# A two-layer decoder on one core: pacing of the routed rows, constant products ahead of the first expert block, and parts of four, three and one groups

## Chip, core and metric

One core of one Trainium2 chip runs the whole program. The metric is the device time of one execution in microseconds (us); three timed runs of the kernel before gave a median of 1179.47 us (1178.01 to 1180.00).

## What is computed

The input is 32 sequences of 128 tokens with 128 features, and a context of 32 x 128 x 96. Six residual steps follow each other; each takes a layer norm of `x` (the fifth norms `x` once more as latents) and adds its result to `x`:

```python
x = x + rope_attention(ln(x))               # 16 heads of 8
x = x + cross_attention(ln(x), ctx)         # 16 heads of 8
x = x + gated_experts(ln(x))                # 8 routed, 2 shared, hidden 64
x = x + causal_attention(ln(x))             # 16 heads of 8
x = x + latent_attention(ctx, ln(x), mask)  # 2 heads of 64
x = x + relu_experts(ln(x))                 # 8 experts of 512, the best two of each token
```

The change touches the last step. For a token, `probs = softmax(xf @ router_w + router_b)`, the two greatest are kept and scaled to a sum of one, and the token's output is the gated sum of the two experts `relu(xf @ w1[e] + b1[e]) @ w2[e] + b2[e]`. All of it is in float32.

## The kernel before

**Groups and slots.** The 32 sequences are 8 groups of 4 (`NG = 4`). The order of the work is written out by hand: `at(slot, phase, fn)` files a function, and one loop over slots runs, in each slot, the phases open, pre, the attention products of that slot, inner, turn, turned, mid and post. Each engine takes its instructions in the order in which this loop emits them; a slot is a place in that order and not a length of time. The three attentions fill slots 0 to 191 (64 slots each, 8 for a group), with a tail of six slots. `done(stage, g)` is the slot in which group g leaves an attention: `8 * (8 * stage + g) + 17`; so `done(2, 3)` is 169 and `done(2, 7)` is 201. The other steps are filed beside the attentions, by offsets from `done`.

**Latent attention** of group g starts at `d = done(2, g) + 2` and its routing at `d + 19`.

**Routing** (`plan_route`) is made by units of two groups, (0,1), (2,3), (4,5), and of one, (6,) and (7,). Logits, choice of two experts, gates and ranks follow in neighbouring slots; `places` (L1707 on, on VectorE) turns ranks into row numbers, and `scatter` (L1729, an indirect DMA that GpSimd issues) writes the 128 rows of one sequence and one choice to a table in DRAM, `slots[f]`, sorted by expert. A unit of two groups has 16 scatters and a unit of one has 8, two in a slot.

**Empty rows.** `preset` (L2057, on SyncE's queue) fills `slots[f]` with rows whose target is out of bounds, long before the scatters: 12 DMAs, one in every fourth slot from slot 4.

**Parts.** The expert step runs in three parts: groups 0 to 3, groups 4 and 5, groups 6 and 7. A part has `NB` blocks of 128 rows (39, 23, 23), and its blocks go in pairs (20, 12, 12), one pair a slot:

- `table` (VectorE) turns the counts of rows into an expert and a row for each block
- `fetch` (L1868, SyncE) loads a block of rows, four pairs ahead; it waits for all scatters of its part
- `weights` (L1877 on ScalarE, L1879 on VectorE) copies the expert's first matrix out of `all_w`, which `keep` loads in 8 x 2 DMAs from slot 203 on
- `turn` (L1887 on PE, L1889 on VectorE) transposes the block
- `hidden` (L1897 on PE, L1903 and L1905) and `result` (L1914 on PE, L1921 and L1923) are the two products with their evictions
- `leave` (L1928, an indirect DMA issued by GpSimd) writes the 128 results to `y[f]` by token
- when a part is over, `gather` (L1943) reads both results of each token of a group, `finish` (L1948 on GpSimd, L1949 on VectorE) adds them to `x`, and `store` (L1568) writes the group out. The last part's groups do this after the last slot.

The parts begin in slots 209, 229 and 241; the first pair's `hidden` is two slots later.

**Constant products.** `awake` (L298) multiplies an identity in bfloat16 by itself, 128 x 512, into a bank of the pool `ps_t`, and nothing reads it. The kernel before has 46 of these, all in its first 41 us. From slot 197 on `ps_t` has no other user until the first `result`.

Of the kernel before, what the change touches and what calls it, by code (L numbers as in the profile page):

```python
# [22 lines left out]
P = 128  # L23
# [3 lines left out]
G = B // NG  # L27
# [5 lines left out]


BLOCK = 128
PARTS = [(0, 1, 2, 3), (4, 5), (6, 7)]
ROOM = [NG * S * len(p) for p in PARTS]
NB = [2 * r // BLOCK + E - 1 for r in ROOM]
SLOTS = [E * r + E * BLOCK for r in ROOM]
# [50 lines left out]
def constants():  # L90
# [8 lines left out]
    token = np.zeros((P, 2, B), np.int32)  # L99
    for p in PARTS:  # L100
        b = np.arange(NG * len(p))
# [12 lines left out]
def decoder(ctx: ExitStack, tc: tile.TileContext, a: dict, out: bass.AP):  # L114
    nc = tc.nc
# [6 lines left out]
    ps_t = ctx.enter_context(tc.tile_pool(name="ps_t", bufs=2, space=PSUM))  # L122
# [6 lines left out]
    def bank(pool):  # L129
        return pool.tile([P, 512], F32, tag="bank", name="bank")  # L130
# [112 lines left out]
    ident_b = cpool.tile([P, P], BF16, tag="ident_b", name="ident_b")  # L243
# [3 lines left out]
    def wide(t, shape, axis):  # L247
        return t.unsqueeze(axis).to_broadcast(shape)
# [1318 lines left out]
    def store(g):  # L1567
        nc.sync.dma_start(out[g * NG : (g + 1) * NG].rearrange("b p d -> p b d"), X[g])  # L1568
# [5 lines left out]

    N2 = 2 * NG
    UNITS = [(0, 1), (2, 3), (4, 5), (6,), (7,)]
    UNITS_OF = [(0, 1), (2,), (3, 4)]

    def router(slots, lazy):
        b2 = cpool.tile([E, D], F32, tag="b2", name="b2")  # L1580
# [7 lines left out]
        def plan_route(at, g, t):  # L1588
# [5 lines left out]
            groups = UNITS[q]  # L1594
            f = next(f for f, units in enumerate(UNITS_OF) if q in units)
            before = e_base[f] if q == UNITS_OF[f][0] else carry[q - 1]
# [111 lines left out]
            def places():  # L1708
                place = tile8("place")
                nc.vector.tensor_tensor(  # L1710
                    place, m["rp"][:, : n2 * E].rearrange("p (b e) -> p b e", e=E), wide(before, [P, n2, E], 1), ALU.add
                )
                nc.vector.tensor_tensor(carry[q], m["rp"][:, n2 * E : (n2 + 1) * E], before, ALU.add)
                at2 = small.tile([P, 2, N2], F32, tag="r_at", name="r_at", bufs=2)
                for c in range(2):
                    t = tile8("t")
                    nc.vector.tensor_tensor(t, m["picks"][:, c], place, ALU.mult)
                    nc.vector.tensor_reduce(at2[:, c, :n2], t, AX.X, ALU.add)
                m["ati"] = small.tile([P, 2, N2], I32, tag="r_ati", name="r_ati", bufs=2)
                nc.vector.tensor_copy(m["ati"][:, :, :n2], at2[:, :, :n2])  # L1720
                for c in range(2):
                    t = tile8("t")
                    nc.vector.tensor_tensor(t, m["picks"][:, c], m["e"], ALU.mult)
                    nc.vector.tensor_reduce(m["rows"][c][:, :n2, D + 1], t, AX.X, ALU.add)
                    nc.gpsimd.tensor_copy(m["rows"][c][:, :n2, D].bitcast(I32), token[:, c, NG * groups[0] : NG * groups[0] + n2])

            def scatter(c, n):
                def fn():
                    ins = nc.gpsimd.indirect_dma_start(  # L1729
                        slots[f], bass.IndirectOffsetOnAxis(ap=m["ati"][:, c, n : n + 1], axis=0), m["rows"][c][:, n, :], None,  # L1730
                        bounds_check=SLOTS[f] - 1, oob_is_err=False,
                    )
                    tc.declare_no_dep(ins.ins, group=f"slots{f}", reason="no two tokens have one slot")
                    tc.add_to_no_dep_group(f"slots{f}", ins.ins)
                return fn
# [34 lines left out]
            def ranks():  # L1770
                gates()
                ranks_pe()
                places()

            def gates_over(u):
                def fn():
# [28 lines left out]
                t += 1  # L1805
            at(t + 6, "mid", choose3)
            at(t + 7, "mid", ranks)
            n = 0
            for k in range(n2):
                for c in range(2):  # L1810
                    at(t + 8 + n // 2, ("pre", "inner")[n % 2], scatter(c, k))
                    n += 1
            for u in us:
                at(t + 8 + u, "mid", gates_over(u))
# [4 lines left out]
    def expert_blocks(f, total, lazy):  # L1819
# [117 lines left out]
        def gather(g):  # L1937
            b = (g - PARTS[f][0]) * NG
            last = g in PARTS[-1]
# [13 lines left out]
    def experts(halves, lazy, heads, late):  # L1953

        def beside(at, done):
            def swap():
                heads.close()
                lazy["blocks"] = late.enter_context(tc.tile_pool(name="blocks", bufs=3, reuse_waits="tile"))

            def keep(e):  # L1960
                def fn():
                    rows = a["w_f"][e * P : (e + 1) * P]
                    if e == 0:
                        for tag, n in (("w1", W1), ("w2", 512)):
                            lazy[tag] = lazy["blocks"].tile([P, E * n], F32, tag=tag, name="all_" + tag, bufs=1)
                    nc.sync.dma_start(lazy["w1"][:, e * W1 : (e + 1) * W1], rows[:, :W1])
                    nc.sync.dma_start(lazy["w2"][:, e * 512 : (e + 1) * 512], rows[:, W1:])
                return fn

            at(done(2, G - 1) + 2, "open", swap)  # L1970
            for e in range(E):
                at(done(2, G - 1) + 2 + e, "open", keep(e))
            begins = [done(2, 3) + 40]
            begins.append(max(begins[0] + (NB[0] + 1) // 2, done(2, 5) + 40))
            begins.append(max(begins[1] + (NB[1] + 1) // 2, done(2, 7) + 33))

            def plan_part(f):
                table, fetch, weights, turn, hidden, result, leave, gather, finish = halves[f]
                t = begins[f]
                pairs = (NB[f] + 1) // 2  # L1980
                at(t - 4, "mid", table)
                for i in range(4):
                    at(t, "post", lambda i=i: fetch(i))
                for i in range(2):
                    at(t + i, "post", lambda i=i: weights(i))
                at(t + 1, "post", lambda: turn(0))
                for i in range(pairs):
                    s = t + 2 + i
                    if i + 1 < pairs:
                        at(s, "pre", lambda i=i: turn(i + 1))  # L1990
                    at(s, "inner", lambda i=i: hidden(i))
                    at(s + 1, "post", lambda i=i: result(i))
                    at(s + 2, "mid", lambda i=i: leave(i))
                    if i + 4 < pairs:
                        at(s, "post", lambda i=i: fetch(i + 4))
                    if i + 2 < pairs:
                        at(s, "post", lambda i=i: weights(i + 2))
                if f + 1 < len(PARTS):
                    for n, g in enumerate(PARTS[f]):
                        at(begins[f + 1] + 6 + 2 * n, "post", lambda g=g: gather(g))  # L2000
                        at(begins[f + 1] + 8 + 2 * n, "post", lambda g=g: finish(g))
                        at(begins[f + 1] + 10 + 2 * n, "post", lambda g=g: store(g))

            for f in range(len(PARTS)):
                plan_part(f)
        return beside
# [46 lines left out]
    def preset(n):  # L2053

        chunks = SLOTS[n // 4] // (2 * P)
        part = slots[n // 4].rearrange("(c p r) w -> p c (r w)", p=P, r=2)[:, n % 4 * chunks // 4 : (n % 4 + 1) * chunks // 4]
        nc.sync.dma_start(  # L2057
            part, nowhere.rearrange("p r w -> p (r w)").unsqueeze(1).to_broadcast([P, chunks // 4, 2 * ROW])
        )

    def once(at, done):

        at(-8, "mid", lambda: folded_bias(w_o0, b_v0, b_o0, bias0))
        at(8, "mid", lambda: nc.gpsimd.memset(z_all, 0.0))
        at(8, "mid", fold_context)
        at(9, "mid", fold_small)
        at(40, "mid", lambda: folded_bias(w_xo0, b_xv0, b_xo0, biasx))
        at(41, "mid", lambda: masked_bias(b_mx, b_xqk0[:, 0:1], b_xqk0[:, 1:2]))
        for n in range(2):
            at(104 + n, "mid", lambda n=n: fold_rotation(2 * n))  # L2070
        at(106, "mid", lambda: masked_bias(b_m1, b_qk1[:, 0:1], b_qk1[:, 2:3]))
        at(107, "mid", lambda: folded_bias(w_o1, b_v1, b_o1, bias1))
        at(108, "mid", lambda: folded_bias(w_xo1, b_vl, b_xo1, bias_l))
        for n in range(4 * len(PARTS)):
            at(4 + 4 * n, "mid", lambda n=n: preset(n))
        guard = []
        at(138, "mid", lambda: guard.append(cross_guard(word)))
        at(140, "mid", lambda: guard[0]())
# [22 lines left out]
    gather, finish = halves[-1][-2:]  # L2101
# [102 lines left out]
```

## Time and profile before

| what | value |
|---|---|
| timed runs, median (lowest, highest) | 1179.47 us (1178.01, 1180.00) |
| the profiled execution, its own time | 1184.79 us |
| its span, first to last instruction | 1183.1 us |
| mean granted TensorE clock | 0.943 |
| PE, VectorE, ScalarE, GpSimd busy | 1067.5, 823.1, 615.8, 645.3 us |
| last attention product (L661) | starts at 864.6 us |
| first `hidden` of part 0, 1, 2 | 928.0, 1063.4, 1119.5 us |
| last `leave` issued | 1166.3 us |
| mean of one `scatter`, one `leave` on GpSimd | 994 ns (64 of them), 1004 ns (85) |

The profile is one execution, so its rows add up to its own 1184.79 us, which is 5.3 us above the median. An engine's rows carry the source line, the operation and "written tile <- read tiles". "Idle before, releaser" is the time for which the engine stood still ahead of an instruction, and who ended that; "issue" is time in which it waited for nothing that the profile shows, and "remote" is a wait whose releaser the profile can't name. PEclk is the share of the full TensorE clock that was granted. A row of the table of stretches is: stretch, its length, and for PE, weight loads, VectorE, ScalarE and GpSimd the busy time with the number of instructions in brackets, then the granted clock, the busy share of the DMA engines and GB/s.

### The profile page before, as it was taken

To read this page: it belongs to the slowest core of one execution; us is meant where nothing else is said; L and a number is where in the kernel's file an instruction comes from. 1 tells how busy PE (TensorE), PEld (TensorE's weight loads), DVE (VectorE), ACT (ScalarE), POOL (GpSimd) and SP (SyncE) were. 2 spreads that over 40 slices of the span, in tenths; PEclk is the share of its full clock that TensorE was granted. 3 is DMA by queue.
4 is the path that set the end of the run, shared out by engine and by line. 5 is a ranking of instruction groups with operands and counts; after the bars stand their busy time and mean duration, and the time that the engine had idled before them with its cause. 6 is when DMAs were issued, how large, how long until landed. Compare 5 with 4: busy or idle time off the path is not lost.

```text
span 1183.1 us, 32419 instructions
## 1 busy us (share of the span) xinstructions
PE 1067.5 (90%) x12495; PEld 829.2 (70%) x12495; DVE 823.1 (70%) x2424; ACT 615.8 (52%) x1440; POOL 645.3 (55%) x918
## 2 busy tenths in 40 slices
PE   6999999999999999999998999989988888788893
PEld 3666667677767776677667677767766778678893
DVE  4678878878778666867787788778666565454652
ACT  2356555676655555554555666744633543333551
POOL 4576656434442544235647675746837245555653
PEclk9999989999999999999999999989976899888997
DMA  8753331000121011110110000001115222123432
GB/s 204 220 154 101 101 100 61 29 29 29 38 47 46 7 41 37 38 26 14 38 46 7 11 15 15 16 11 35 31 37 157 69 56 58 38 66 86 107 109 77
DMA packets 77858, 71.24 MB, mean 60 GB/s; under 512 B 14554, under 2 KB 66829, under 8 KB 77696
## 3 DMA queue, kind: packets, MB, share of 16 engines
q1 hardware_dynamic: 72640, 60.08, 18.7%
q0 software_dynamic: 4768, 8.47, 2.1%
q8 instruction: 102, 1.67, 0.6%
q10 hardware_dynamic: 288, 0.52, 0.1%
q14 instruction: 60, 0.49, 0.1%
HBM read 33.39 MB, written 37.02 MB: 60 GB/s over the span
## 4 chain that ended last, share of the span: by engine, by line
PE 52%; DVE 19%; POOL 10%; ACT 7%; issue 6%; DMA 4%; SPq 0%; another core or an unknown queue 0%; DVEq 0%; POOLq 0%; ACTq 0%
PE bank L633 11%; PE bank L1897 5%; PE bank L661 5%; PE bank L1914 5%; DVE msc L636 5%; PE bank L950 3%; DMA g<-spread 3%; POOL h L941 2%; ACT e L644 2%; PE bank L1121 2%; PE bank L511 1%; PE bank L932 1%; DVE qa L540 1%; PE bank L1200 1%; PE bank L1226 1%
## 5 line engine op out<-in xcount | busy, mean ns | idle before, releaser
L644 ACT ACTIVATE e<-bank 128x512 f32<-128x512 f32 x384 | 207.6, 593 | 178.5 <-PE bank L633 174.2
L636 DVE TENSOR_REDUCE msc<-bank 128x4 f32<-128x512 f32 x384 | 245.2, 680 | 70.1 <-PE bank L633 67.1
L633 PE MATMUL bank<-kb,qz 32*128 32x256 f32 x1536 | 243.8, 410 | 12.3 <-DVE msc L636 10.5
L633 PE MATMUL bank<-qa,kb 32*128 32x128 f32 x3072 | 235.9, 289 | 4.5 <-ACT e L644 4.5
L633 PEld LDWEIGHTS bank<-qa,kb 32*128 32x128 f32 x3072 | 196.6, 191 | 9.7 <-ACT e L644 8.8
L633 PEld LDWEIGHTS bank<-kb,qz 32*128 32x128 f32 x1536 | 146.8, 190 | 65.1 <-DVE msc L636 33.2
L1928 POOL DMA_INDIRECT y<-bo,bx x85 | 85.3, 1004 | 81.5 <-ACT bo L1921 44.0
L647 POOL TENSOR_SCALAR_AFFINE_SELECT e<-e 128x512 f32<-128x512 f32 x128 | 79.2, 642 | 69.5 <-ACT e L644 69.2
L661 PE MATMUL bank<-e,vt 128*32 128x128 f32 x3072 | 109.3, 284 | 0.5 <-POOL e L647 0.5
L1897 PE MATMUL bank<-bxT,w 128*128 128x128 f32 x680 | 92.1, 287 | 9.9 <-issue 9.4
L1897 PEld LDWEIGHTS bank<-bxT,w 128*128 128x128 f32 x680 | 85.9, 202 | 12.5 <-issue 12.0
L1914 PE MATMUL bank<-all_w,bh 128*128 x680 | 91.3, 289 | 3.6 <-issue 3.5
L661 PEld LDWEIGHTS bank<-e,vt 128*32 128x32 f32 x3072 | 81.5, 113 | 15.7 <-POOL e L647 1.5
L1914 PEld LDWEIGHTS bank<-all_w,bh 128*128 128x128 f32 x680 | 85.6, 204 | 6.0 <-issue 5.7
L1729 POOL DMA_INDIRECT slots<-rows,r_ati x64 | 63.6, 994 | 34.0 <-issue 18.4
L1905 DVE TENSOR_SCALAR bh<-bank,w 128x128 f32<-128x128 f32 x164 | 46.1, 343 | 43.8 <-remote 19.6
L941 POOL TENSOR_TENSOR h<-h,g 128x512 f32<-128x512 f32 x30 | 38.7, 1298 | 68.9 <-DMA g<-spread 58.3
L338 ACT ACTIVATE xn<-x,ln_nb,ln_rs 128x128 f32<-128x128 f32 x96 | 42.0, 492 | 49.9 <-POOL ln_nb L332 49.3
L1903 ACT ACTIVATE bh<-bank,w 128x128 f32<-128x128 f32 x176 | 50.3, 368 | 19.9 <-remote 7.7
L1207 ACT ACTIVATE le<-bank,lmx 128x256 f32<-128x256 f32 x64 | 26.9, 471 | 64.7 <-DVE lmx L1206 60.3
L540 DVE SCALAR_TENSOR_TENSOR qa<-bank,head_rows,qz 128x128 f32<-128x128 f32 x192 | 57.6, 342 | 0.0
L1921 ACT ACTIVATE bo<-bank,bx 128x128 f32<-128x128 f32 x44 | 16.2, 368 | 76.2 <-PE bank L1914 47.8
(337 smaller groups left out, 2320.5 us busy)
## 6 DMA issues: line engine op xcount, KB each, us to landing
slots<-nowhere SPq DMA_DIRECT2D x8, 1170.0 KB
slots<-nowhere SPq DMA_DIRECT2D x4, 2210.0 KB
g<-spread SPq DMA_DIRECT2D x16, 512.0 KB
bx<-slots SPq DMA_DIRECT2D x85, 65.0 KB
kv<-kcv SPq DMA_DIRECT2D x8, 516.0 KB
lkv<-kv SPq DMA_DIRECT2D x32, 129.0 KB
yg<-y SPq DMA_DIRECT2D x14, 256.0 KB
all_w<-in_w_f SPq DMA_DIRECT2D x8, 258.0 KB
```

Of the source, the lines that this page charges most:

```text
L540: nc.vector.scalar_tensor_tensor(s["qa"][:, u, :], s["mp"], head_rows[:, 1 - u : 2 - u], m["qz"][:, u, i * P : (i + 1) * P], ALU.mult, ALU.add
L633: nc.tensor.matmul(o, l, r, start=start, stop=stop, skip_group_check=True)
L636: nc.vector.tensor_reduce(tops(MSC[bb % 4], 2 * h + j), sc[j].rearrange("p (s n k) -> p s n k", s=2, n=2), AX.X, ALU.max, negate=True)
L644: nc.scalar.activation(e.rearrange("p n q -> p (n q)"), tr[j], AF.Exp, scale=SCALE)
L647: nc.gpsimd.affine_select(out=e, in_=e, compare_op=ALU.is_ge, fill=0.0, base=0, pattern=[[0, 4], [1, P]], channel_multiplier=-1)
L661: nc.tensor.matmul(s3["av"][32 * n : 32 * n + 32, h3 * P : (h3 + 1) * P], m3["vt"][:, i3, h3, n, u, :], es[u][:, n, :], start=(h3 == 0 and ...
L941: engine.tensor_tensor(m["h"][:, c, :], m["h"][:, c, :], m["g"][:, c, :], ALU.mult)
L1729: ins = nc.gpsimd.indirect_dma_start(slots[f], bass.IndirectOffsetOnAxis(ap=m["ati"][:, c, n : n + 1], axis=0), m["rows"][c][:, n, :], Non ...
L1897: nc.tensor.matmul(ps[:, c * P : (c + 1) * P], w[:, c * P : (c + 1) * P], s["xT"][:, u * P : (u + 1) * P], start=True, stop=True)
L1903: nc.scalar.activation(h, p, AF.Relu, bias=bias)
L1914: nc.tensor.matmul(ps[:, u * P : (u + 1) * P], s["h"][:, u, c, :], lazy["w2"][:, bass.ds(at_w + c * P, P)], start=(c == 0), stop=(c == 3),)
L1928: ins = nc.gpsimd.indirect_dma_start(y, bass.IndirectOffsetOnAxis(ap=x[:, D : D + 1].bitcast(U32), axis=0), s["o"][:, u, :], None, bounds_ ...
```

## The change

Five edits, all in the order of the work; every token and every weight is computed as before.

1. The parts are groups 0 to 3, groups 4 to 6 and group 7: `NB` is 39, 31, 15, in 20, 16 and 8 pairs. They begin in slots 209, 230 and 246.
2. For units of two groups `places` moves from slot t + 7, mid, to t + 8, pre, and the scatters start one slot later. For units of one group there is one scatter in a slot instead of two.
3. The empty rows are written in every eighth slot from slot 20, at the end of the slot, instead of every fourth from slot 4.
4. Three constant products in each of the slots 197 to 210, 42 in all.
5. After a part is over, its groups are gathered, added and stored one slot apart instead of two.

```diff
-PARTS = [(0, 1, 2, 3), (4, 5), (6, 7)]
+PARTS = [(0, 1, 2, 3), (4, 5, 6), (7,)]
...
-    UNITS_OF = [(0, 1), (2,), (3, 4)]
+    UNITS_OF = [(0, 1), (2, 3), (4,)]
...
             def ranks():
                 gates()
                 ranks_pe()
-                places()
+                if len(groups) == 1:
+                    places()
...
+            if len(groups) > 1:
+                at(t + 8, "pre", places)
             n = 0
             for k in range(n2):
                 for c in range(2):
-                    at(t + 8 + n // 2, ("pre", "inner")[n % 2], scatter(c, k))
+                    if len(groups) > 1:
+                        at(t + 9 + n // 2, ("pre", "inner")[n % 2], scatter(c, k))
+                    else:
+                        at(t + 8 + n, "pre", scatter(c, k))
                     n += 1
...
+            begins = [done(2, 3) + 40]
+            begins.append(max(begins[0] + (NB[0] + 1) // 2, done(2, 6) + 37))
+            begins.append(max(begins[1] + (NB[1] + 1) // 2, done(2, 7) + 37))
+
+            def awake():
+                nc.tensor.matmul(
+                    bank(ps_t).rearrange("p (n k) -> p n k", n=4), ident_b, wide(ident_b, [P, 4, P], 1), start=True, stop=True
+                )
+
+            for k in range(done(2, G - 1) - 4, begins[0] + 2):
+                for phase in ("open", "inner", "post"):
+                    at(k, phase, awake)
...
-            begins = [done(2, 3) + 40]
-            begins.append(max(begins[0] + (NB[0] + 1) // 2, done(2, 5) + 40))
-            begins.append(max(begins[1] + (NB[1] + 1) // 2, done(2, 7) + 33))
...
-                        at(begins[f + 1] + 6 + 2 * n, "post", lambda g=g: gather(g))
-                        at(begins[f + 1] + 8 + 2 * n, "post", lambda g=g: finish(g))
-                        at(begins[f + 1] + 10 + 2 * n, "post", lambda g=g: store(g))
+                        at(begins[f + 1] + 5 + n, "post", lambda g=g: gather(g))
+                        at(begins[f + 1] + 6 + n, "post", lambda g=g: finish(g))
+                        at(begins[f + 1] + 7 + n, "post", lambda g=g: store(g))
...
-            at(4 + 4 * n, "mid", lambda n=n: preset(n))
+            at(20 + 8 * n, "post", lambda n=n: preset(n))
```

## The prediction

> **What bounds the kernel now.** I read the busy times first, then the table of 40 slices, the chain that ended last, a table of stretches for the expert step, and the timelines where it is slow.
>
> ```profile
> PE 1067.5 (90%) x12495; PEld 829.2 (70%) x12495; DVE 823.1 (70%) x2424; ACT 615.8 (52%) x1440; POOL 645.3 (55%) x918
> ...
> PE   6999999999999999999998999989988888788893
> ...
> PEclk9999989999999999999999999989976899888997
> ...
> PE 52%; DVE 19%; POOL 10%; ACT 7%; issue 6%; DMA 4%; SPq 0%; another core or an unknown queue 0%; DVEq 0%; POOLq 0%; ACTq 0%
> ```
>
> PE is the bound, but its row drops from 9 to 8 and 7 from slice 28 on, and the clock to 7 and 6 at 860 to 930 us. All five edits but one act there. The next view is the table of stretches.
>
> ```profile
> 900.00:910.00 10.00, 8.46 (x36) 5.72 (x36) 6.74 (x23) 4.35 (x11) 7.87 (x14) 0.50 0.69 196
> ...
> 1010.00:1020.00 10.00, 6.34 (x36) 4.63 (x35) 0.46 (x2) 1.14 (x4) 7.57 (x9) 0.90 0.18 53
> 1020.00:1030.00 10.00, 7.16 (x35) 6.20 (x36) 5.14 (x21) 2.70 (x8) 3.66 (x5) 0.59 0.07 22
> ...
> 1130.00:1140.00 10.00, 10.00 (x92) 10.00 (x91) 5.77 (x18) 6.40 (x18) 5.26 (x6) 1.00 0.61 178
> ```
>
> The last row is what a slot of the expert step costs undisturbed: PE full, and the starts of successive `hidden` are 3.79 us apart. At 1010 to 1020 us PE issues 36 matmuls where it could issue 90, VectorE and ScalarE stand, and GpSimd alone is busy. The timelines of GpSimd and PE there:
>
> ```profile
> 1014.54 0.97 POOL L1729 DMA_INDIRECT slots<-rows,r_ati  x1 [0.30 <-issue]
> 1015.81 0.97 POOL L1729 DMA_INDIRECT slots<-rows,r_ati  x1 [0.30 <-issue]
> ...
> 1015.45 0.27 PE L1914 MATMUL bank<-all_w,bh 128*128 x1 [1.04 <-issue]
> ...
> 1022.62 0.37 PE L1897 MATMUL bank<-bxT,w 128*128 128x128 f32 x1 [1.08 <-issue]
> ```
>
> One indirect DMA costs GpSimd 0.97 + 0.30 = 1.27 us. While eight or more follow without a gap, PE issues one matmul about every 0.7 us, and waits for nothing that the trace names. The same stands at 983, 1035 and 1065 us, and ends with the burst. The DMA engines are busy for only 0.07 to 0.18 there, so they aren't full. I take the bursts as the cause; that is an inference from the coincidence.
>
> **1. Constant products, and the scatters of (2,3) a slot later: -3.5 us.** Between 860 and 933 us the granted clock is half in four stretches (861 to 868, 881 to 888, 892 to 912, 922 to 933). The chain of waits has 26.4 us of PE work in half-clock time; at full clock it would be 13.2, so at most 13.2 us can go. The price: 42 products. The same product in the first 41 us is in the chain as 12 in 2.60 us, 0.217 us each at full clock (4 in 1.82, 0.455 each, at half), so 42 x 0.217 = 9.1 us. PE is idle for 12.1 us of these 70 (70 less the stretches' 57.9); since the products come in order and can't choose the gaps, I let half hide, 4.5, and 4.6 is left. The gain is bounded once more: part 0 starts when the last scatter, issued at 914.65, has landed; the fetches below begin, and 10.8 us later (blocks, `weights`, turn) is the first `hidden`, 928.0. GpSimd's own work from the moment the rows stand, 878 to 881, is 16 x 1.275 and some 9 us more, 29.6; with 2.1 us for the landing of the last, `hidden` can't be earlier than 881 + 29.6 + 2.1 + 10.8 = 923.5. So the most is 4.5 us. The scatters start a slot later, but the slots ahead get shorter. Bounds: -4.5, and +11.7 (all 9.1 on the path, no clock gained, 2.6 us for the slot). I take -3.5, near the GpSimd limit, because the half clock (13.2) is worth more than the price (4.6).
>
> ```profile
> 914.65 0.97 POOL L1729 DMA_INDIRECT slots<-rows,r_ati  x1 [0.30 <-issue]
> ...
> 917.25 6.25 SPq L1868 DMA_DIRECT2D bx<-slots  x8
> ```
>
> ```profile
> 17.95 2.60 PE bank L298 x12
> ```
>
> The first row of the stretches speaks against this edit: PE is busy for 8.46 of 10 us and still gets 0.50. The Trainium skill, "TensorE: Matmul & The Clock Gate", section "Part 1: The HAM clock gate", says that the clock is halved after an idle window of about 3.4 us and released by a busy one. [...] By the page's words nothing would be gained and 4.6 us paid, 8 us above my sum.
>
> **2. Pacing: -13 us.** Before, a slot of the expert step has two leaves and, in slots 216 to 225 and 230 to 233, two scatters of a unit, in 222 and 223 four. GpSimd needs 4 x 1.275 = 5.1 us or 7.65, PE 3.79. By the starts of `hidden`, slots 223 and 224 take 20.8 us where 219 to 222 take 5.2 each (10.4 more), 227 takes 10.5 where its neighbours take 4.6 (5.9 more), 230 to 233 24.5 against 4 x 3.8 (9.3 more); 25.6 together. After, slots 222 to 224 have five indirect DMAs, 225 to 237 three, 3.83 us, about PE's 3.79. I take (first) 10.4 to 5, as slots 217 to 224 stay crowded; (second) 5.9 to 2.6; (third) 9.3 to 4; and 0.04 x 16 = 0.6 for the slots that GpSimd now sets. That is 25.6 - 11.6 - 0.6 = 13.4, rounded down to 13. Bounds: -25.6 (all), and +9 if GpSimd, now never ahead for 21 slots, stalls eight slots more by what slots 230 to 233 cost (9.3). Between them I go by slots 225, 228 and 231 (3.8, 3.7 and 4.2 us), which lie beside fewer indirect DMAs.
>
> **3. Parts of 4, 3 and 1: +3.5 us.** Blocks (85) and pairs (44) are as many; the last pair goes one slot later, since slot 231 has no `hidden`: the pipeline of turn, `hidden`, eviction and `result` runs dry once, one product of 1.79 us. Part 1 now needs group 6's rows. Their last scatter is in slot 229, and the fetch waits for its landing, by the row below 2.11 us, and then some 4.7 us for bx, turn and copy: 6.8 of the 14 us (three and a half slots of 4) to the first product in slot 232, which leaves 7. GpSimd's lag behind PE was some 8 us at its worst (its `leave` of slot 233 at 1075.3). So I add 1.7. Bounds: 0 and +12 (a lag twice as long). Group 7's rows (slot 237) have nine slots to slot 246.
>
> ```profile
> 1076.70 2.11 DMA slots<-rows,r_ati
> ```
>
> Three tables, three first fetches and as many `weights` remain. Fetches wait on SyncE, so a late scatter also holds the gathers and stores queued behind; these are not needed before the end.
>
> **4. The end: -2.0 us.** Two groups were left after the last block; now one.
>
> ```profile
> 1169.09 4.03 DMA yg<-y
> 1173.24 2.54 POOL L1948 TENSOR_TENSOR yg<-yg 128x512 f32<-128x512 f32 x2 [5.97 <-DMA yg<-y]
> 1174.53 2.40 DVE L1949 TENSOR_TENSOR x<-x,yg 128x512 f32<-128x512 f32 x2 [10.67 <-POOL yg L1948]
> ```
>
> The second GpSimd add (1.27) goes, and its VectorE add with it: the last one, from 1176.93, ends where the first does, 1175.2; that is 1.7, and half a us of the gathers (2 instead of 4). The three `finish` of part 1 in slots 252 to 254 cost GpSimd 2 x 1.27 + 1.29 = 3.84 us in a slot of 3.79: +0.2. Bounds: -3 and +2 (a GpSimd late by one add and one DMA).
>
> **5. Empty rows: 0.** They lie under the attentions, where no DMA is on the chain before 360 us; the slots 8 to 48 take 3.4 to 3.9 us and 48 to 64 3.3, with other loads in the first, so some of that may come back or move. Bounds -2 and +2. The last is issued in slot 108 and its rows are needed from slot 175 on.
>
> **Sum:** -3.5 - 13 + 3.5 - 2 + 0 = -15. Against the profiled run, 1184.8 to 1169.8; against the median, 5.3 lower, 1179.5 to **1164.5 us**. I let the difference of the two stand.
>
> **Rivals.** *Pacing is worth nothing* (A): three indirect DMAs in a slot leave GpSimd as busy as four in fewer slots, the same 64 scatters stall PE for the same sum. For it: the stall may be by DMA and not by burst (64 x 1.27 is 81 us). Against: at 988 to 993 and 994.8 to 999.6 four without gap cost nothing. The sum is -3.5 + 0.6 + 2 - 2 = -3, about 1176.5. *The clock stays* (B): the products are paid at 4.6 and nothing is gained; +4.6 - 13 + 3.5 - 2 = -7, 1172.5. *Part 1 waits for group 6* (C, slower): the bursts stay and GpSimd reaches slot 229 late; from 7 us of lag on, each further us is one us of PE in slot 232. With 15 us of lag, twice before's worst less a little: 8 us. The pacing then brings nothing: -3.5 + 0 + 2 + 8 - 2 = +4.5, 1184. It decides the sign from a lag of 10.5 us on. For it speaks that slots 217 to 229 hold 24 scatters and 24 leaves, 48 x 1.275 + 4 = 65 us, while PE needs 68 at the undisturbed 5.2 a slot with its other work: nearly a tie.
>
> **How the numbers follow.** Forecast 0.5, A 0.2, B 0.1, C 0.2. 0.2% of the time, 2.4 us, is about what a measurement of this kernel can tell from no change. A lies half in this, half under it. So faster 0.5 + 0.1 + 0.1 = 0.70, same 0.10, slower 0.20. The range goes from 1152 (-4.5, -20, 0, -3) to C's 1184.
>
> **What would show it.** Right: clock near 1.0 in 900 to 930 us and the first `hidden` at 923 to 925 instead of 928.0; starts of `hidden` under 5 us apart in slots 225 to 237, and no stretch with 36 matmuls in 10 us after 1025; part 1's first `hidden` less than 9 us after part 0's last; last GpSimd add x1. Wrong: half clock at 900 to 912 still; a PE that waits, in slot 232, for the fetch and that for `slots<-rows`; matmuls 0.7 us apart in slots with three indirect DMAs.

## The result, and the profile after

The changed kernel is **slower**: 1184.52 us median (8 runs) beside 1177.95 us for the kernel before (8 runs), ratio 1.0051, 95% interval 1.0032 to 1.0070. The forecast was 1164.5.

The profiled execution of the changed kernel took 1182.13 us (span 1180.3), less than its median, as that of before (1184.79) took more than its own. The two traces can therefore not simply be subtracted; their stages can be compared. The page after:

```profile
PE 1060.6 (90%) x12537; PEld 821.3 (70%) x12537; DVE 820.8 (70%) x2424; ACT 616.0 (52%) x1440; POOL 647.2 (55%) x918
...
PE   6989999999999999999998999989888888778993
...
PEclk9899999999999999999999999999988898898997
...
PE 53%; DVE 16%; POOL 11%; issue 8%; ACT 7%; DMA 3%; another core or an unknown queue 1%; SPq 1%; POOLq 0%; DVEq 0%; ACTq 0%
```

The 42 products are there (12537 matmuls, before 12495), and the clock in slices 30 and 31 is 8 and 8 where it was 7 and 6. But the PE row still falls to 8 and 7, and "issue" has grown from 6 to 8%. The table of stretches, in the columns of before:

```profile
900.00:910.00 10.00, 8.21 (x40) 5.96 (x40) 6.12 (x22) 4.66 (x12) 7.94 (x9) 0.69 0.50 153
1010.00:1020.00 10.00, 4.34 (x21) 3.61 (x20) 1.43 (x5) 0.91 (x4) 6.52 (x7) 0.77 0.16 53
...
1060.00:1070.00 10.00, 4.05 (x19) 4.06 (x20) 1.87 (x4) 2.52 (x7) 6.24 (x7) 0.50 0.31 66
```

Two stretches have some 20 matmuls in 10 us where an undisturbed one has 90: the stalls are still there. The last group's end is as it was meant to be, one addition on GpSimd and one on VectorE:

```profile
1172.58 1.26 POOL L1954 TENSOR_TENSOR yg<-yg 128x512 f32<-128x512 f32 x1 [5.85 <-DMA yg<-y]
1173.87 0.69 DVE L1955 TENSOR_TENSOR x<-x,yg 128x512 f32<-128x512 f32 x1 [11.69 <-POOL yg L1954]
```

**Four chips.** The runs below came in five groups, each on one chip beside the kernel before; in order the chips were numbers 12, 12, 0, 13 and 10. The kernel before took 1147.4 and 1150.0 us on chip 12 and 1146.1 on chip 10, but 1178.8 on chip 0 and 1178.9 on chip 13. I call chips 0 and 13 stalling and chips 12 and 10 quiet. The chip of the first measurement isn't on record; by its time and its stages it was a stalling one. That the chip makes the difference is read from the fact that each group agrees in itself. Only kernels of one group are compared by time; a ratio is always to the kernel before on the same chip.

**Stages.** The traces are cut at the first softmax exponential (L644) of slot 184, and at starts of `hidden`, counted by pairs from 0 to 43 (pairs 0 to 19 are part 0). Pair k is in slot 211 + k, in the changed kernel from pair 20 on in slot 212 + k. All in us, of one profiled execution:

| kernel, chip | to pair 0 | 0 to 5 | 5 to 15 | 15 to 19 | 19 to 21 | 21 to 43 | to the end | sum |
|---|---|---|---|---|---|---|---|---|
| before, stalling | 100.6 | 30.7 | 74.5 | 24.9 | 9.6 | 92.5 | 23.0 | 355.7 |
| after, stalling | 102.2 | 31.3 | 73.7 | 24.3 | 16.8 | 88.4 | 21.8 | 358.5 |
| after_third, stalling | 100.6 | 31.2 | 73.0 | 25.6 | 16.4 | 87.0 | 21.3 | 355.2 |
| before_again, quiet | 96.0 | 33.2 | 53.4 | 23.1 | 9.5 | 84.7 | 23.2 | 323.1 |
| after_again, quiet | 100.1 | 31.0 | 52.6 | 21.3 | 10.4 | 86.6 | 21.4 | 323.3 |

Slot 184 itself begins at 818 to 830 us in these and the other traces, of one kernel at 818.1 and 827.2; that spread isn't the change's.

### The profile page after: what moved, and what is told of

It is laid out like the page before. It is cut to its first block, busy times and chain, and to the rows that moved or that the text cites. A ratio compares the mean times of both kernels' runs of the same rounds, so it can differ in the third digit from the quotient of the medians.

```text
span 1180.3 us, 32496 instructions
## 1 busy us (share of the span) xinstructions
PE 1060.6 (90%) x12537; PEld 821.3 (70%) x12537; DVE 820.8 (70%) x2424; ACT 616.0 (52%) x1440; POOL 647.2 (55%) x918
## 4 chain that ended last, share of the span: by engine, by line
PE 53%; DVE 16%; POOL 11%; issue 8%; ACT 7%; DMA 3%; another core or an unknown queue 1%; SPq 1%; POOLq 0%; DVEq 0%; ACTq 0%
PE bank L633 12%; PE bank L1903 5%; PE bank L661 5%; PE bank L1920 5%; DVE msc L636 5%; PE bank L950 3%; POOL h L941 2%; PE bank L932 2%; POOL slots L1729 2%; PE bank L933 2%; ACT e L644 2%; PE bank L511 1%; POOL e L647 1%; PE bank L486 1%; DMA g<-spread 1%
## 5 line engine op out<-in xcount | busy, mean ns | idle before, releaser
L644 ACT ACTIVATE e<-bank 128x512 f32<-128x512 f32 x384 | 207.6, 593 | 175.5 <-PE bank L633 170.5
L633 PE MATMUL bank<-kb,qz 32*128 32x256 f32 x1536 | 242.5, 408 | 12.3 <-DVE msc L636 10.4
L633 PE MATMUL bank<-qa,kb 32*128 32x128 f32 x3072 | 234.6, 288 | 4.5 <-ACT e L644 4.5
L1729 POOL DMA_INDIRECT slots<-rows,r_ati x64 | 63.2, 988 | 25.4 <-issue 21.8
L1927 ACT ACTIVATE bo<-bank,bx 128x128 f32<-128x128 f32 x44 | 16.2, 369 | 76.5 <-PE bank L1920 31.3
```

Source lines behind the costliest of these rows:

```text
L633: nc.tensor.matmul(o, l, r, start=start, stop=stop, skip_group_check=True)
L644: nc.scalar.activation(e.rearrange("p n q -> p (n q)"), tr[j], AF.Exp, scale=SCALE)
L1729: ins = nc.gpsimd.indirect_dma_start(slots[f], bass.IndirectOffsetOnAxis(ap=m["ati"][:, c, n : n + 1], axis=0), m["rows"][c][:, n, :], Non ...
```

## Experiments

**Each edit alone, on chip 12, a quiet one.** First the kernel before as it is, then one edit at a time (for `awake_only` the loop of edit 4, for `presets_only` the line of edit 3, for `pace_only` edit 2, for `parts_only` edits 1 and 5; `all_but_parts` has 2, 3 and 4).

> The kernel before, unchanged: a second profile of it, and five more timed runs. The first profiled execution took 1184.8 us, 6.8 above the median of eight runs, and its attentions reached slot 112 5.6 us later than the changed kernel's. If that was one slow execution, this profile is near 1178, slots 96 to 112 take 75 us as in the changed kernel, and the bursts of the expert step stall less. If a profile adds time, it is near 1185 again.

1147.95 us in the profiled run, median 1148.56, 30 us under the first measurement. Slot 184 comes 4.3 us earlier than in the first profile; the other 33 us of the difference lie behind it, 21 of them in pairs 5 to 15. GpSimd's timeline there, and the stretch:

```profile
997.12 0.97 POOL L1729 DMA_INDIRECT slots<-rows,r_ati  x1 [0.30 <-issue]
998.40 0.97 POOL L1729 DMA_INDIRECT slots<-rows,r_ati  x1 [0.30 <-issue]
999.68 0.97 POOL L1729 DMA_INDIRECT slots<-rows,r_ati  x1 [0.30 <-issue]
```

```profile
990.00:1000.00 10.00, 10.00 (x88) 9.74 (x87) 7.97 (x27) 4.64 (x14) 7.13 (x8) 1.00 0.23 66
```

The same gapless run of indirect DMAs (13 in a row up to 1007 us, later 21 from 1030.9 to 1057.5), at the same 0.97 + 0.30, and PE full beside the first and busy for 25.0 of 26.5 us beside the second. Bursts alone do not stall this chip.

> The kernel before with the 42 constant products alone. Theory 1 (the clock was worth it, and the loss is elsewhere): -4 to -6 us, more than the 4.0 us that the changed kernel's profile shows at the first hidden, since here the scatters stay ahead of the key norms. Theory 2 (the products fill PE where it is busy): +3 to +6. Half clock should be gone from 880 to 900 us.

Ratio 1.0007 (0.9984 to 1.0030). Half clock between slot 184 and pair 0 falls from 30.8 to 15.3 us, and pair 0 comes 97.0 after slot 184 instead of 96.0. Theory 1 of the products falls; theory 2's +3 lies at the upper end of the interval (+3.4 us). The middle is about nothing.

> The kernel before with the empty rows of the same parts written in every eighth slot from slot 20. Theory 1: 0 +-2. Theory 3 (the loss of the changed kernel is in the attentions, where large writes now stand beside the loads of slots 84 to 112): +4 to +7, with the loss at slots 20 to 112 in its profile.

1.0003 (0.9979 to 1.0027). Theory 3 falls.

> The kernel before with edit 2 alone: scatters of units of two one slot later, those of units of one one in a slot, parts as before. My prediction's step 2: -13 (less 2.6 for the first block's delay). Rival A: 0. The changed kernel's profile says that 20 us stalls at slots 222 to 226 remain; by it 0 to -5, and the first hidden 2 to 3 us later than in the kernel before.

1.0002 (0.9978 to 1.0026). To pair 0 98.9 (+2.9 on before_again), pairs 15 to 19 20.6 instead of 23.1 (-2.5): the two halves of the edit cancel.

> The changed kernel, unchanged, beside the kernel before on one chip. The runs just made had no stalls in the expert step although GpSimd's bursts were longer (23 indirect DMAs in a row), and the kernel before took 1147 us instead of 1178. If the loss of 6.6 us is in the part boundary and the places, it is the same here: +3 to +7. If it was a matter of the stalls, 0 +-2 here, and +6 where the stalls are.

0.9983 (0.9954 to 1.0012): on this chip the change is no difference that can be measured.

> The kernel before with edits 1 and 5 alone: parts of 4, 3 and 1 groups, begun in slots 209, 230 and 246, and one slot between the gathers; scatters two a slot as before. Theory 1 (the boundary costs, and it is what makes the changed kernel slower): +4 to +7, with a stop of 5 us or more about slot 232 and -1.3 at the end. Theory 4 (it is the pacing with the parts: group 6's rows come late only when they are paced): -1 to +2 here.

0.9989 (0.9961 to 1.0017). Pairs 19 to 21 take 9.1 (before 9.5), 21 to 43 86.9 (84.7), the end 22.3 (23.2). No stop at the boundary.

> Edits 2, 3 and 4 with the parts of before. Theory 1: 0 +-2, as each of the three alone was within 0.1% of the kernel before. If together they cost (the products and the later places both stand ahead of part 0): +3 or more.

1.0005 (0.9973 to 1.0036); to pair 0 100.1, as in the whole change.

**Fewer scatters.** The scatters of groups 4 to 7 go, and with them what would read rows never written:

```diff
-                    at(t + 8 + n // 2, ("pre", "inner")[n % 2], scatter(c, k))
+                    if groups[0] < 4:
+                        at(t + 8 + n // 2, ("pre", "inner")[n % 2], scatter(c, k))
...
         def gather(g):
+            if f:
+                return
...
         def finish(g):
+            if f:
+                return
```

> The kernel before without the 32 scatters of groups 4 to 7 and without the gathers and additions of parts 1 and 2, so that the tables of these parts stay empty and x misses their results. It asks whether GpSimd's bursts cause the stalls. If they do, and the chip is one that stalls, slots 217 to 234 take 3.8 to 5.2 us each, some 25 us less than in the first profile. If they don't, matmuls 0.7 us apart remain at slots 218, 224, 228 or 233. On a chip without stalls: only slot 227 (10 us) may shrink.

On chip 12, a quiet one, 1133.01 us (two runs), 17 less than before; 11 of it is the end (12.0 instead of 23.2), and pairs 5 to 15 stay at 53.6. So it said nothing on stalls yet.

**The later slot of units of two, undone.** The next group was on chip 0, a stalling one. `pace_no_shift` is the kernel before with one scatter a slot for units of one; `after_no_shift` is the changed kernel with

```diff
-                if len(groups) == 1:
-                    places()
+                places()
...
-            if len(groups) > 1:
-                at(t + 8, "pre", places)
...
                     if len(groups) > 1:
-                        at(t + 9 + n // 2, ("pre", "inner")[n % 2], scatter(c, k))
+                        at(t + 8 + n // 2, ("pre", "inner")[n % 2], scatter(c, k))
                     else:
                         at(t + 8 + n, "pre", scatter(c, k))
```

> The kernel before with half of edit 2: units of one group scatter one a slot, but the units of two keep their places and scatters. On a chip without stalls, by the stages of the traces so far (from slot 184 to the first hidden, 96 before and 98.9 with the whole of edit 2): the first hidden 96 +-1.5 after slot 184, last scatter of (2,3) at 82 to 84; then pairs 15 to 17 in 11.8 instead of 14.3. In all -2 to -3 us (0.2%) against the kernel before. If the shift is not what delays part 0, 98.9 stays. On a chip with stalls: rival A (pacing is worth nothing) says 0 to -3, my step 2 says -13.

0.9979 (0.9958 to 1.0001). Pairs 5 to 15 take 70.6: of the 21 us that they take more in the first profile than on the quiet chip, 17 stay, and pairs 15 to 19 even take 28.3 instead of 24.9. My step 2 (-13) falls, rival A (nothing) stands.

> The changed kernel without the shift of the units of two (places and scatters of (0,1), (2,3), (4,5) as before), all else as changed. By the stages: first hidden 97 after slot 184 instead of 100.1, so 3 us less than the changed kernel and 2 to 4 less than the kernel before. If the products, and not the shift, delay part 0, 100 stays.

0.9981 (0.9963 to 0.9999). The whole change wasn't run on this chip; it had 1.0051 (1.0032 to 1.0070) at first and, below, 1.0021 (1.0003 to 1.0039) on chip 13. The intervals just don't meet, if ratios of different stalling chips may be compared. To pair 0 99.3 instead of 102.2 and 100.6.

> As the run before it, with part 0's and part 1's gathers, additions and stores two slots apart as in the kernel before (edit 5 undone). By the stages pairs 21 to 43 take 86.6 with edit 5 and 84.7 to 85.5 without: 1 to 2 us less, some 4 us under the kernel before. If the three later finishes crowd the end (slots 254 to 258), the tail grows by 1 to 3 us instead.

1.0054 (1.0030 to 1.0079), 8.8 us above the run before it where 1 to 2 less were expected. The end takes 23.7 instead of 21.6 (the alternative I had named), pairs 15 to 21 41.7 instead of 39.1, 21 to 43 90.5 instead of 88.6. Edit 5 is worth its place on this chip, more than the one term I gave it; why the stalls grow with it undone isn't shown.

> As the run before it, without the constant products. By the stages they cost 1.0 before part 0 and gain 0 to 2 behind it: -1 to +1 against the run before it, with 24 to 44 us of half clock between slots 184 and 211 instead of some 14. Theory 1 of the products (the half clock is worth 4 us) says +4.

1.0032 (1.0009 to 1.0055), 1.4 us under the run before it, within both intervals. Half clock before pair 0 33.8 us against 15.0, and pair 0 at 98.7 against 99.8. Again the clock comes back and the time doesn't.

**What makes the stalls.** `no_late_scatters_2` is the kernel above again; `double_leaves` adds to it, in `leave`:

```diff
+        y_more = tc.dram_tile([2 * room, D], F32, name=f"y_more{f}")
...
+                ins = nc.gpsimd.indirect_dma_start(
+                    y_more, bass.IndirectOffsetOnAxis(ap=x[:, D : D + 1].bitcast(U32), axis=0), s["o"][:, u, :], None,
+                    bounds_check=2 * room - 1, oob_is_err=False,
+                )
...
```

> The kernel without the 32 scatters of groups 4 to 7 and without the gathers and additions of parts 1 and 2, a second time: x misses the results of parts 1 and 2. On the chip without stalls it took 1133 us, its pairs 5 to 15 53.6 us, 15 to 17 9.7. If this is the chip that stalls and GpSimd's density or the scatters cause the stalls (theories 5 and 6): again about 1133, pairs 5 to 15 in 53 to 56 instead of 70 to 74. If neither (theory 7): 1160, pairs 5 to 15 in 70 or more.

Chip 13, a stalling one (before 1178.9): 1140.84 us (two runs), ratio 0.9672 (0.9626 to 0.9718). Pairs 5 to 15 take 53.5 as on the quiet chip; pairs 12 and 13, which took 8.6 and 12.3 us in the first profile, take 5.1 and 3.8. The 10 us that stalled are full, though by now they hold pairs 13 to 15:

```profile
1010.00:1020.00 10.00, 9.84 (x87) 9.54 (x86) 7.98 (x29) 5.69 (x16) 7.91 (x12) 1.00 0.08 27
```

Theory 7 falls: the stalls go with the scatters, or with the density.

> The run before it, and each leave twice, the second into a table that nothing reads: four indirect DMAs a slot through the whole expert step and no scatter after part 0's. x misses the results of parts 1 and 2 as above. On a chip without stalls slots take 4 x 1.275 = 5.1 us once GpSimd is the bound. If density makes the stalls (theory 5), slots from 217 on, where the chip stalls, have matmuls 0.7 us apart and slots of 8 to 12 us. If it is the scatters (theory 6), an even 5.1.

1233.14 us (two runs), 1.0455 (1.0416 to 1.0493). Pairs 5 to 15 take 71.7, 21 to 43 130.7 (22 slots of 5.1 would be 112), with no scatter behind pair 0. A stretch, and the timeline of such a stall ("remote" is a wait whose releaser isn't named):

```profile
1100.00:1110.00 10.00, 5.98 (x37) 5.54 (x37) 3.66 (x14) 3.18 (x10) 6.19 (x7) 0.83 0.01 0
```

```profile
1101.28 0.97 POOL L1930 DMA_INDIRECT y<-bo,bx  x1 [0.30 <-issue]
1102.56 0.97 POOL L1936 DMA_INDIRECT y_more<-bo,bx  x1 [0.30 <-issue]
1102.84 1.14 ACT L1905 ACTIVATE bh<-bank,w 128x128 f32<-128x128 f32 x4 [4.69 <-remote]
...
1105.01 1.13 DVE L1907 TENSOR_SCALAR bh<-bank,w 128x128 f32<-128x128 f32 x4 [6.01 <-remote]
```

GpSimd goes on, ScalarE and VectorE stand for 5 to 6 us, as in the first profile. Theory 6 falls: the stalls need no scatter. Theory 5, density, stands on this chip: four a slot stall, two hardly. Nor is it the bytes: this stretch lies in part 1, whose table is empty, so that its leaves have no row to write; the DMA engines are busy for 0.01 of it and move 0 GB/s, and the stall is there. What remains is the issuing itself, and by which way it holds up the other engines isn't shown. The kernel wasn't run on a quiet chip.

> The changed kernel once more, for a second profile beside these. On the chip that stalls +0.3 to +0.7% (first measurement +0.51%) and 13 us at slots 230 to 232; on the other 0 +-0.3% and 8 us.

On chip 13 1.0021 (1.0003 to 1.0039): slower, by less than at first. Slot 230 takes 13.0 us, as expected.

**The last group** came on chip 10, a quiet one. `sparse_last_group` is `after_no_shift` with

```diff
+                    elif groups[0] == 7:
+                        at(t + 8 + 2 * n, "pre", scatter(c, k))
```

> after_no_shift with the scatters of group 7 in every second slot (230 to 244) instead of every slot: 2.5 indirect DMAs a slot, 3.2 us of GpSimd in 3.8. Where the chip stalls, theory 5 (density) says that slots 232 to 241 take 3.8 us each, up to 5 us less than in after_no_shift (58 us from slot 230's hidden to slot 244's there). On a chip without stalls the same as after_no_shift within 1 us.

0.9938 (0.9915 to 0.9961): 1140.12 us beside 1146.05, 0.6% below the kernel before, and more than expected. Its stages sum to 320.5 (before_again 323.1, after_again 323.3): pairs 15 to 19 18.7, 21 to 43 84.2. The other 3 us of the median no stage shows. `after_no_shift` wasn't run on a quiet chip, so how much of this the sparser scatters bring isn't shown; and on a stalling chip this kernel wasn't run, so whether 2.5 a slot is sparse enough there stays open.

> The whole of edit 2 alone, a second time. On the chip that stalls pace_no_shift was 0.2% under the kernel before; if the later slot of the units of two costs there what it costs on the other chip (2.9 us before the first hidden) or more, this is +1 to +6 us. If the shift costs nothing there: -2.

0.9999 (0.9972 to 1.0026), to pair 0 98.9, as at first.

> Edits 1 and 5 alone, a second time. On the other chip -0.1 +-0.3%. On the chip that stalls, part 1 waits for group 6's rows (rival C): +3 to +8 us with 13 us from slot 230 to 232. If the boundary is only the one empty slot: 0 to +2.

0.9978 (0.9953 to 1.0002). To pair 0 it took 101.1, the same kernel 95.4 before: half clock for 46.7 us against 27.4. Over the ten traces with neither the products nor the later slot, this stage took 95.4 to 97.9 us where 22 to 31 us of it were at half clock, and 98.7 to 101.3 where 34 to 47 were: the clock does weigh there. With the products alone half clock is down to 15 to 22 us, and the stage takes 97.0 to 99.8; with products and later slot 100.1 to 102.2.

## Why the prediction was wrong, by its steps

**Step 2, pacing: -13 forecast, about nothing measured.** This is the step that failed. "I take the bursts as the cause" held on the stalling chips: 53.5 instead of 74.5 for pairs 5 to 15 without the late scatters, and stalls all along with doubled leaves. What failed is what the step built on it: that with the scatters of groups 6 and 7 thinned, three stalls would shrink by 5.4, 3.3 and 5.3 us and nothing else would grow. All in us, between starts of `hidden`:

| slots | before | forecast | pace_no_shift | after | after_third |
|---|---|---|---|---|---|
| 223 and 224 | 20.9 | 15.5 | 16.4 | 19.3 | 19.0 |
| 227 | 10.6 | 7.3 | 11.7 | 7.9 | 10.1 |
| 230 to 233 | 24.5 | 19.2 | 21.2 | other parts | other parts |
| pairs 0 to 43 | 232.1 | 218.7 | 232.2 | 234.6 | 233.2 |

What the three places gained came back elsewhere. In `pace_no_shift` slot 220 takes 10.7 us instead of 5.1 and slot 237 6.4 instead of 3.8; in the changed kernel slot 221 takes 9.0 and 8.3 instead of 5.6 and slot 230 13.1 and 13.0 instead of 5.4. Beside the quiet chip (203.9 before, 201.9 after) the stalls in pairs 0 to 43 cost 28 us before and 31 to 33 after.

The load was not made sparse. Groups 4 and 5 keep two scatters a slot, so the changed kernel has four or five indirect DMAs in each of the slots 217 to 224, and some 20 of its 31 to 33 us of stalls lie in pairs 5 to 15. GpSimd's two longest runs without a gap in the expert step were of 13 and 10 indirect DMAs before and are of 12 and 7 after. The slots that got three leave no pause either, by the sum's own figures: 3.83 us of GpSimd in a slot of 3.79, for which it charged 0.6 us. That a pause is what was missing there is argued; shown is that two a slot hardly stall.

Rival A (0.2) had this mechanism. Its price, 1176.5, is for the whole change, which took 1184.5. The row I set against it, four in a row at 988 us without cost, was a short burst and not the density over several slots.

**Step 1, products and the later scatters: -3.5 forecast; 0 to +2 on stalling chips, +4.1 between the two quiet traces.** Half clock ahead of pair 0 falls from 39.8 to 14.4 us, but pair 0 comes at 100.6 before and at 102.2 and 100.6 after. The chain that ended last doesn't name one engine for this stage (855 to 925 us): PE has some 56% of it in `before` and 50% in `after_no_shift`, but only some 11% in `after` and in `presets_only`, which has no products; there GpSimd's work has some 30% and "issue" over a third. I read this as a near tie of PE and GpSimd; measured is that relieving PE alone brought no time (`awake_only`, 1.0007). In all the traces pair 0 follows the last scatter of (2,3) by 12.9 to 14.3 us. I had that bound, and counted GpSimd's work from the moment the rows stand. They stood at 877.2 us, but with the scatters a slot later another instruction is ahead of them in GpSimd's queue, and waits:

```profile
866.46 0.32 POOL L1725 COPY rows<-token 128x8 int32<-128x8 int32 x2
881.38 1.67 POOL L1139 TENSOR_TENSOR nrml<-nrml,half 128x8 f32<-128x8 f32 x1 [14.60 <-DVE nrml L997]
883.23 1.12 POOL L1729 DMA_INDIRECT slots<-rows,r_ati  x1 [0.18 <-POOL nrml L1139]
```

Before, two scatters were out ahead of that wait:

```profile
878.50 1.12 POOL L1729 DMA_INDIRECT slots<-rows,r_ati  x1 [6.30 <-DVE rows L1724]
879.92 0.98 POOL L1729 DMA_INDIRECT slots<-rows,r_ati  x1 [0.30 <-issue]
887.72 1.68 POOL L1139 TENSOR_TENSOR nrml<-nrml,half 128x8 f32<-128x8 f32 x1 [6.82 <-DVE nrml L997]
```

And "the slots ahead get shorter" hardly held: counted from slot 184, that wait ends at 59.6 us after and at 60.3 before. So GpSimd is idle for 14.6 us and then has sixteen scatters to issue. On quiet chips `pace_only` came to pair 0 at 98.9 us twice, 2.9 behind `before_again`, in a stage that varies by as much with the clock. On stalling chips the change without the shift is 0.2% under the kernel before, with it, on other chips, 0.2 to 0.5% over. It is the only edit that was taken out of the whole change alone, so that it makes the change slower is likely and not shown to the end.

The rule of the Trainium skill that I set against this step ("TensorE: Matmul & The Clock Gate", section "Part 1: The HAM clock gate") would have the clock released by busy windows; the half clock did shrink with the products. My estimate by its words, nothing gained in clock, was wrong in the clock, and its +4.6 us lie nearer to the measured 0 to +4.1 than my -3.5 do.

**Step 3, the boundary: +3.5 forecast.** Quiet: pairs 19 to 21 10.4 instead of 9.5, +0.9, and +1.9 in pairs 21 to 43. No wait for group 6's rows. On stalling chips it took 16.8 and 16.4 instead of 9.6, but that is a stall: GpSimd works, ScalarE, VectorE and then PE stand.

```profile
1060.46 0.97 POOL L1934 DMA_INDIRECT y<-bo,bx  x1 [0.30 <-issue]
...
1065.40 0.37 ACT L1927 ACTIVATE bo<-bank,bx 128x128 f32<-128x128 f32 x1 [7.57 <-remote]
1065.47 0.42 DVE L1895 COPY bxT<-bank 128x256 f32<-128x256 f32 x1 [3.35 <-remote]
1065.95 0.69 PE L1893 MATMUL bank<-ident,bx 128*128 128x128 f32 x2 [6.96 <-DVE bxT L1895]
```

Pairs 21 to 43 are 4 to 5.5 us shorter: the stall of before in slot 232 (10.4 us) is gone. Rival C, the slower one, had the place right and the mechanism wrong: SyncE's fetch had begun at 1050.98. That its 1184 is the measured time is luck.

**Step 4, the end: -2.0 forecast.** 23.0 to 21.8 and 21.3, and 23.2 to 21.4: right. The +0.2 for part 1's three additions doesn't show: pairs 40 to 42 take 3.8, 3.7 and 3.6 us in `before_again` and `after_again` alike. What the sum left out are part 0's four additions, which edit 5 also puts one slot apart: beside them pairs 25 to 28 take 18.8 us instead of 16.9 on the quiet chip, the 1.9 of step 3.

**Step 5, empty rows: 0 forecast, 1.0003 (0.9979 to 1.0027) measured.** Right.

**The signs.** The first `hidden` came at 924.0, inside the 923 to 925 that were to show the forecast right, but by luck: slot 184 began 5.6 us earlier than in the profile of before. The clock at 900 to 930 us was 0.69, 1.00 and 0.83, not near 1.0; starts of `hidden` are 7.9 us apart at slot 227 and 13.1 at 230; and 1060 to 1070 us has 19 matmuls. The last addition x1 came as said.

**What stays open.** The stages of the stalling chips' traces sum to 355.7 before, 358.5 and 355.2 after; the medians say +2.9 to +6.6. Only one trace of before is from a stalling chip, and it is of an execution above its median, so the last 2 to 5 us have no place. Nor is it shown what the stalling chips have that the quiet ones haven't.

## To carry to other kernels

Thinning part of a load need not remove a stall: here it moved to the slots that stayed crowded and to those whose thinned load still filled them (3.83 us in 3.79). Compare the thinned rate with the slot it must fit, over all the slots around it, before counting on a gain. Work that is moved one slot later goes behind whatever its engine has queued there; read that engine's queue, not only when its inputs are ready. Before raising the clock of an engine ask what bounds the stage beside it: here PE got its clock back, GpSimd's scatters came no earlier, and the time stayed. And measure a kernel beside the one it is compared with on one chip, and on more than one chip.

## What was not expected of the hardware

One kernel took 1146 to 1150 us on two chips and 1179 on two others; between the two profiles 28 of some 33 us lie between pairs 0 and 43, where a slot has up to six indirect DMAs. On a quiet chip 21 of them without a gap left PE busy for 25.0 of 26.5 us. On stalling chips four a slot made ScalarE, VectorE and PE stand for some 5 to 10 us at a time while GpSimd went on at 1.27 us each, even where the DMAs moved 0 GB/s.
